# A two-layer graph network on one core: the search for low halves in the second batch, and the last batch's steps placed anew

## The chip, the cores and the metric

The kernel runs on one core of a Trainium2 chip. The metric is the device time of one launch in microseconds (us). One execution was recorded by the hardware profiler; all stretches of time in this document come from such records.

The names of the engines: PE is TensorE (matrix products), DVE is VectorE, ACT is ScalarE, POOL is GpSimd, and SP is SyncE, which here only issues DMA transfers. Each has its own queue of instructions and works through it in order.

## The reference

There are 32 batches of 512 rows with 512 columns, one 512x512 adjacency matrix of zeros and ones, and two layers, each followed by a residual and a normalisation of the rows.

```python
# layer 0: masked attention, 8 heads of 64
q = x @ Wq + bq; k = x @ Wk + bk; v = x @ Wv + bv
scores = einsum('bihd,bjhd->bhij', q, k) / sqrt(64) + where(adj == 0, -1e9, 0)
x = layernorm(x + einsum('bhij,bjhd->bihd', softmax(scores), v))
# layer 1: aggregation over neighbours, then a product
y = einsum('nm,bmd->bnd', adj, x)
x = layernorm(x + einsum('bnd,do->bno', y, weight) + bias)
```

## The kernel before, in words

All products of 512x512 matrices with a weight are made from seven products of halves instead of eight (a Strassen-like scheme: `FACTORS`, `ORDER`, L353 in `block_product`). One such product is one unit: `project(b, "q"/"k"/"v", i)` for the projections and `convolve(b, i)` for the product with the second layer's weight. A unit has 8 matmul records on PE, and its bank of PSUM is drained by DVE or ACT. Seven units make a whole product. Some of the sums of halves that go into them (`combine_rows`, L318) are made on POOL.

Attention runs in groups of four heads, two groups to a batch. For each group `attend` (L576) makes the weighted sum of values, `fold_squares` (L609, L611) adds up the exponentials on DVE, and `turn_out` (L592, L597) transposes the result on DVE into a tile named attT (two buffers) and sends it by 16 small DMA transfers into a tile of rows. `scores` (L552, L554, L556, L567) makes the scores of the next group: PE, then DVE adds the mask, ACT takes the exponential, POOL adds exponentials up. `scale_rows` (L635, ACT, 8 instructions for one pair of heads) and `add_rows` (L639, POOL) bring the result into the rows of x. In the last group of the last batch there are no rows by DMA: ACT copies into attT (L589), and `last_residual` (L645, L646, L648) turns it on PE and adds it on DVE.

The second layer takes y from the normalised rows. Each row tile is split into a high and a low half of reduced precision (L441 and L445; for the last batch by rows, `split_rows`, L486 on ACT and L487 on DVE), PE multiplies both with the adjacency (L472, for the last batch L499 in `aggregate_rows`), and ACT and DVE copy the banks to the tile yT (L475, L477; last batch L506, L504, L508). The adjacency itself must survive a reduction to the high half. `look_for_low_half` tests it, one block of rows at a time: ACT copies (L294) to a tile named high, DVE compares (L296) into a tile named attT, and reduces (L297). At the end `judge` joins this with two other measures (sums of exponentials and their inverses, gathered for each group by `add_up`), PE adds the verdict over the partitions (L864), and if it is bad, a general kernel runs after the fast one. With these inputs it does not run.

`statistics` (L415, L416) takes mean and variance of a block of 128 rows on DVE, `square_root` (L419, ACT), `invert_root` (L424, L425, DVE) and `normalise` (L430, ACT, one block of rows an instruction) make the normalisation. The last batch takes the statistics of the second layer by half rows (`half_statistics`, L837, closed in L854).

The order of work is written out by hand. `units_of(b)` returns two lists for a batch, one behind each of its groups of attention. `merge(units, behind)` places a list of small steps behind each PE unit: the k-th entry of `behind` follows the k-th unit. Work of four batches is in flight at once: while batch b is in attention, batch b+1 is projected, batch b-1 gets its first normalisation, splits and aggregation, and its second product comes up to a batch later; b-2 gets its second normalisation. After the loop over groups, a section written by hand ends the last two batches: t is B-1 = 31, `rest` the seven convolution units of t-1, `last` those of t. The order of the seven units is always 1, 2, 5, 6, 7, 3, 4.

Some tiles have few buffers, and a new use waits for the last reader of the old one: attT has two, high and low two each, k and q two each, yT one. Before, in the last batch, blocks 0 to 3 of `split_rows` share the two buffers of high and low. The unit `convolve(b, 7)` adds into the same MIX tile that unit 6 filled and that POOL reads.

Of the kernel before, what the change touches and what calls it, by code (L numbers as in the profile page):

```python
# [37 lines left out]
FP = mybir.dt.float32  # L38
FR = mybir.dt.float32r
# [168 lines left out]
def fast_kernel(ctx: ExitStack, tc, verdict, x, adj, Wq, bq, Wk, bk, Wv, bv, W1, b1, out):  # L208
# [3 lines left out]
    HP = H // 2  # L212
    NB = N // P
    DB = D // P
    assert N == 512 and D == 512 and H * HD == D
    root = float(HD) ** 0.5

    consts = ctx.enter_context(tc.tile_pool(name="consts", bufs=1))
# [199 lines left out]
    def square_root(t, slots):  # L418
        nc.scalar.activation(RSTD[t][:, slots], STAT[t][:, slots, 1], AF.Sqrt, bias=eps)  # L419

    def invert_root(t, slots):

        rstd = RSTD[t][:, slots]
        nc.vector.reciprocal(rstd, rstd)  # L424
        nc.vector.scalar_tensor_tensor(SHIFT[t][:, slots], STAT[t][:, slots, 0], -1.0, rstd,  # L425
                                       op0=ALU.mult, op1=ALU.mult)
# [25 lines left out]
    def store(b, blocks=None):  # L452
        for c in blocks or ():
            nc.sync.dma_start(out[b, c * P:(c + 1) * P, :], X[b][:, c, :])
        if blocks is None:
            nc.sync.dma_start(out[b].rearrange("(c p) d -> p c d", p=P), X[b])
# [23 lines left out]

    def split_rows(b, c):

        high = HIGH[b, c] = work.tile([P, D], FR, name="high")
        low = LOW[b, c] = work.tile([P, D], FR, name="low")
        row = X[b][:, c, :]
        nc.scalar.activation(high, row, AF.Copy)  # L486
        nc.vector.tensor_sub(low, row, high.bitcast(FP))  # L487

    def add_bias(b, c):
        nc.vector.tensor_add(X[b][:, c, :], X[b][:, c, :], b1_r)  # L490

    def aggregate_rows(b):

# [17 lines left out]
    def convolve(b, i):  # L511

        pm = bank(2, half)
        block_product(pm, YT[b], w1, i)
        x11, x12, x21, x22 = (X[b][:, 2 * r:2 * r + 2, s * half:(s + 1) * half] for r in range(2) for s in range(2))
        if i == 1:

            MIX[b] = work.tile([P, 2, half], FP, name="mix", tag="q" if b >= B - 3 else "low", bufs=2)
            nc.scalar.activation(MIX[b], pm, AF.Copy)
        if i in (6, 7):  # L520
            nc.vector.tensor_add(MIX[b], pm, MIX[b])
            for block in (x12,) if i == 6 else (x21, x22) if b == B - 1 else (x22,):
                nc.gpsimd.tensor_add(block, block, MIX[b])
        for block in {1: (x11,), 5: (x12, x22), 2: (x11,), 3: (x12,), 4: (x21,)}.get(i, ()):
            nc.vector.tensor_add(block, pm, block)  # L525
        if i == 4 and b < B - 1:

            nc.gpsimd.tensor_add(x21, x21, MIX[b])
# [6 lines left out]
    def convolution(b):  # L535
        return [(convolve, b, i) for i in (1, 2, 5, 6, 7, 3, 4)] if b >= 0 else []
# [104 lines left out]
    def last_residual(b, hp):  # L641

        pt = bank(NB, 2, HD)
        for c in range(NB):
            nc.tensor.transpose(pt[:, c, :, :], AT[b, hp][:, c * P:(c + 1) * P], ident)  # L645
        nc.vector.tensor_mul(pt, pt, inverse_of(b, hp)[:, :, :, None].to_broadcast([P, NB, 2, HD]))  # L646
        cols = X[b][:, :, hp * P:(hp + 1) * P]
        nc.vector.tensor_add(cols, pt.rearrange("p c s d -> p c (s d)"), cols)  # L648
# [15 lines left out]
    def run(units):  # L664
        for unit in units:
            unit[0](*unit[1:])
# [46 lines left out]
    def norm(t, which):  # L713

        if t - which < 0:
            return []
        lo, hi = which * NB, (which + 1) * NB
        return [(square_root, t, slice(lo, hi)), (invert_root, t, slice(lo, hi))] + [
            (normalise, t, slot) for slot in range(lo, hi)]
# [4 lines left out]
    def survey(b):  # L724

        return [(statistics, b, 1, c) for c in range(NB)] if b >= 0 else []
# [5 lines left out]
    def merge(units, behind):  # L732

        merged = []
        for k in range(max(len(units), len(behind))):
            merged += units[k:k + 1] + (behind[k] if k < len(behind) else [])
        return merged

    def units_of(b):

        made, turned = projections(b + 1), flips(b + 2)
        splits, gathered = aggregation(b - 1)
        old, seen = norm(b - 1, 1), survey(b - 2)

        fresh, young = ([(statistics, b - 1, 0, c) for c in range(NB)], norm(b - 1, 0)) if b else ([], [])
        scaled, added = residuals(b, 0)
        if b == B - 1:


            first, second = folds(b, 1)  # L750
            behind = [fresh[:2], fresh[2:], young[:1], young[1:3], young[3:5] + [first], young[5:] + splits[:1],
                      splits[1:]]
            return [merge(convolution(b - 2), behind), [second] + merge(gathered, [scaled, added, seen[:2], seen[2:]])]

        ready = [(turn_over, b)] if b > 1 else []
        if old:
            behind = [seen[:2], seen[2:], old[:2], old[2:4] + fresh[:2], old[4:] + ready + fresh[2:]] + [
                [u] for u in young]
        elif b:
            behind = [ready + fresh] + [[u] for u in young]  # L760
        else:
            behind = [[]] + [[(sum_weights, w1, n)] for n in range(4)]
        behind += [[] for _ in range(11 - len(behind))]
        behind += [splits[:1], scaled + added, splits[1:2]]
        slot0 = merge(made[:16], behind)
        values = made[16:]
        looked = [(look_for_low_half, c) for c in range(NB)] if b == 0 else []
        scaled, added = residuals(b, 1)
        slot1 = values[:3] + looked[:2] + gathered[:1] + splits[2:3] + gathered[1:2] + splits[3:] + scaled[:1]
        slot1 += values[3:] + looked[2:]  # L770
        if b == B - 2 > 0:
            slot1 += [(load, B - 1)]
        slot1 += gathered[2:3] + turned[:1] + gathered[3:]
        convolved = convolution(b - 1) if b < B - 2 else []
        slot1 += merge(convolved, [scaled[1:] + added[:1] + turned[1:2], turned[2:3], turned[3:4], [], [], [],
                                   added[1:] + turned[4:]])
        return [slot0, slot1]
# [31 lines left out]
    rest, last = convolution(t - 1), convolution(t)  # L809
    for hp in range(HP - PAIRS, HP):  # L810
        last_residual(t, hp)
    run(rest[:1])
    old, seen = norm(t - 1, 1), survey(t - 1)
    run(old[:1] + rest[1:2] + old[1:])
    if t > 1:
        store(t - 2)

    for c in range(NB):
        statistics(t, 0, c)
    ahead = norm(t, 0)  # L820
    run(ahead[:1] + rest[2:3] + ahead[1:2])
    for c in range(NB):
        run(ahead[2 + c:3 + c] + rest[3 + c:4 + c])
        split_rows(t, c)
    run(rest[3 + NB:])
    for c in range(NB):
        add_bias(t, c)
    aggregate_rows(t)


    halves = {}
# [2 lines left out]
    def half_statistics(c, s):  # L834
        if c not in halves:
            halves[c] = spare[:, c, :, :]
        nc.vector.bn_stats(halves[c][:, s, :], X[t][:, c, s * half:(s + 1) * half])  # L837

    old = norm(t, 1)
    beside = {1: seen, 2: old[:2], 5: old[2:3], 6: old[3:5], 7: old[5:]}  # L840
    for unit in last:
        run([unit] + beside.get(unit[2], []))
        if unit[2] == 2:
            well = judge()
        if unit[2] == 7 and t > 0:
            store(t - 1)
        for c, s in {2: ((0, 0), (1, 0)), 3: ((0, 1), (1, 1)), 4: ((2, 1), (3, 1), (2, 0), (3, 0))}.get(unit[2], ()):
            half_statistics(c, s)
            if (c < 2) == (s == 1):
                if t + 1 not in STAT:  # L850
                    for table, name, shape in ((STAT, "stat", (2 * NB, 2)), (RSTD, "rstd", (2 * NB,)),
                                               (SHIFT, "shift", (2 * NB,))):
                        table[t + 1] = work.tile([P, *shape], FP, name=name, bufs=3)
                nc.vector.bn_aggr(STAT[t + 1][:, NB + c, :], halves[c])  # L854
        ready = {3: (0, 1), 4: (2, 3)}.get(unit[2], ())
        if ready:
            slots = slice(NB + ready[0], NB + ready[1] + 1)
            square_root(t + 1, slots)
            invert_root(t + 1, slots)
            for c in ready:  # L860
                normalise(t + 1, NB + c)
                store(t, [c])
    pm = bank(N)
    nc.tensor.matmul(pm[0:1, 0:1], well, ones[:, 0:1], start=True, stop=True)  # L864
    nc.vector.tensor_scalar(verdict, pm[0:1, 0:1], P - 0.5, None, op0=ALU.is_lt)


# [22 lines left out]
```

## Time and profile before

| what | us |
|---|---|
| median of 3 runs (2759.68 to 2760.57) | 2759.97 |
| the profiled execution | 2760.76 |
| its span from first to last instruction | 2758.2 |
| PE busy | 2733.3 |
| POOL busy | 1898.7 |
| DVE busy | 2065.3 |
| ACT busy | 1411.5 |
| transfers of x and rows: SP issues an attT transfer, median until it lands | 1.8 |

A line of a timeline gives: start, duration, engine, line of the kernel, instruction, what is written and read with the shapes, how many instructions were merged, and in brackets how long the engine idled ahead of it and which event ended that. A line of waits gives: engine, tile and line that waited, for whom, then us in total, how many times, the longest. A line of stretches gives: from and to, length, busy us and number of instructions of PE, PE's weight loads, DVE, ACT and POOL, then the mean TensorE clock granted (1.00 is full), the share of the DMA engines and GB/s.

### The profile page before, as it was taken

Reading aid. Unit: us, or ns where it says so; the run is one execution under the profiler, and the core shown is the slowest. Engines: PE = TensorE matmul, PEld = TensorE weight load, DVE = VectorE, ACT = ScalarE, POOL = GpSimd, SP = SyncE. Lnnn points to the kernel's source line nnn. Section 1 sums busy time; section 2 is a strip of 40 time slices with the busy share of each in tenths; the row PEclk is TensorE's granted clock in tenths of the full one; section 3 lists DMA queues with packets and bytes.
Section 4 is the critical chain, followed back from the end, with each engine's and each line's share of the span. In section 5 each row is a group of like instructions: output and inputs, shape, how many; then the busy total and the mean of one; then the engine's idle time right before and its main releaser. Section 6 shows DMA issues by size and latency. Waiting matters only on the chain.

```text
span 2758.2 us, 39360 instructions
## 1 busy us (share of the span) xinstructions
PE 2733.3 (99%) x12856; PEld 1912.9 (69%) x12856; DVE 2065.3 (75%) x3351; ACT 1411.5 (51%) x2460; POOL 1898.7 (69%) x1220
## 2 busy tenths in 40 slices
PE   9999999999999999999999999999999999999997
PEld 6676766767767667677676676776766767767665
DVE  6778777777777777777877777777777777787777
ACT  3455554654545545446555465454554544655554
POOL 4666776767776668676677676777666867667774
PEclk9999999999999999999999999999999999999999
DMA  5112212222112222122221222211222212222111
GB/s 148 29 31 59 57 19 54 59 61 56 26 48 57 62 57 44 30 56 61 59 57 18 55 59 61 56 27 47 58 62 57 44 30 56 61 59 57 24 52 49
DMA packets 592915, 142.20 MB, mean 52 GB/s; under 512 B 554560, under 2 KB 558656, under 8 KB 592704
## 3 DMA queue, kind: packets, MB, share of 16 engines
q1 hardware_dynamic: 592704, 139.63, 22.9%
q8 instruction: 103, 1.69, 0.3%
q14 instruction: 108, 0.88, 0.1%
HBM read 72.88 MB, written 33.55 MB: 39 GB/s over the span
## 4 chain that ended last, share of the span: by engine, by line
PE 97%; DVE 1%; SPq 1%; ACT 0%; DMA 0%; issue 0%; POOL 0%; DVEq 0%; ACTq 0%
PE bank L353 55%; PE bank L552 16%; PE bank L576 16%; PE bank L472 8%; SPq L597 1%; PE bank L619 0%; DMA wq<-in_L_gnn_Wq_dram 0%; DVE bnst L415 0%; ACT rows L635 0%; PE bank L499 0%; DVE xT L525 0%; DVE part L837 0%; DVE xs L525 0%; DVE xT L490 0%; DVE stat L416 0%
## 5 line engine op out<-in xcount | busy, mean ns | idle before, releaser
L556 ACT ACTIVATE e<-e 128x1024 f32<-128x1024 f32 x512 | 524.5, 1052 | 579.8 <-DVE e L554 545.0
L554 DVE SCALAR_TENSOR_TENSOR e<-gap,bank 128x512 f32<-128x512 uint8 x1024 | 617.8, 678 | 20.6 <-PE bank L552 20.6
L567 POOL TENSOR_TENSOR es<-es,e 128x1024 f32<-128x1024 f32 x256 | 618.7, 2417 | 20.1
L567 POOL TENSOR_TENSOR es<-e 128x1024 f32<-128x1024 f32 x128 | 315.8, 2467 | 334.2 <-ACT e L556 334.2
L552 PE MATMUL bank<-q,k 64*128 64x512 f32 x2048 | 463.6, 598 | 0.0
L576 PE MATMUL bank<-e,v 128*64 128x512 f32 x2048 | 456.5, 598 | 4.7 <-DVE v L388 4.7
L353 PE MATMUL bank<-wv,xT 128*128 128x256 f32 x1792 | 405.4, 381 | 0.0
L353 PE MATMUL bank<-xT,wq 128*128 128x256 f32 x1792 | 400.8, 381 | 2.2 <-DMA wq<-in_L_gnn_Wq_dram 1.8
L353 PE MATMUL bank<-xT,wk 128*128 128x256 f32 x1792 | 402.9, 379 | 0.0
L353 PE MATMUL bank<-w,yT 128*128 128x256 f32 x1792 | 392.3, 379 | 0.5 <-DVE yT L504 0.5
L552 PEld LDWEIGHTS bank<-q,k 64*128 64x128 f32 x2048 | 203.1, 186 | 258.9 <-issue 149.2
L353 PEld LDWEIGHTS bank<-w,yT 128*128 128x128 f32 x1792 | 340.0, 190 | 48.3 <-DVE yT L504 0.9
L353 PEld LDWEIGHTS bank<-xT,wk 128*128 128x128 f32 x1792 | 340.2, 190 | 46.1
L353 PEld LDWEIGHTS bank<-xT,wq 128*128 128x128 f32 x1792 | 337.8, 190 | 49.1 <-issue 2.0
L353 PEld LDWEIGHTS bank<-wv,xT 128*128 128x128 f32 x1792 | 337.5, 190 | 47.6 <-DVE e L554 0.8
L635 ACT ACTIVATE rows<-rows,zero,inverse 128x64 f32<-128x64 f32 x1008 | 343.3, 426 | 0.0
L576 PEld LDWEIGHTS bank<-e,v 128*64 128x64 f32 x2048 | 142.2, 137 | 283.8 <-issue 282.7
L639 POOL TENSOR_TENSOR xs<-xs,rows 128x512 f32<-128x512 f32 x124 | 158.6, 1290 | 164.9 <-DMA xs<-in_x_dram 164.9
L556 ACT ACT_TABLE_LOAD x30 | 38.5, 1283 | 423.9 <-DVE e L554 423.9
L445 DVE TENSOR_TENSOR low<-xs,high 128x512 fp32r<-128x512 f32 x122 | 143.3, 1174 | 104.1 <-ACT high L441 104.1
L430 ACT ACTIVATE xs<-xs,shift,rstd 128x512 f32<-128x512 f32 x248 | 181.9, 803 | 32.3 <-DVE shift L425 32.3
L525 DVE TENSOR_TENSOR xs<-bank,xs 128x512 f32<-128x512 f32 x186 | 124.4, 683 | 97.0 <-PE bank L353 46.6
(123 smaller groups left out, 2963.5 us busy)
## 6 DMA issues: line engine op xcount, KB each, us to landing
rows<-attT SPq DMA_DIRECT2D x2016, 16.0 KB, 1.8
xin<-in_x_dram SPq DMA_DIRECT2D x496, 64.0 KB, 2.4
xs<-in_x_dram SPq DMA_DIRECT2D x31, 1024.0 KB, 5.1
out_dram<-xs SPq DMA_DIRECT2D x31, 1024.0 KB, 4.4
xin<-in_x_dram SPq DMA_DIRECT2D x4, 256.0 KB, 3.5
wq<-in_L_gnn_Wq_dram SPq DMA_DIRECT2D x2, 512.0 KB, 7.0
wk<-in_L_gnn_Wk_dram SPq DMA_DIRECT2D x2, 512.0 KB, 5.1
yT<-in_adj_dram SPq DMA_DIRECT2D x1, 1024.0 KB, 8.3
```

The source lines that it names most:

```text
L353: nc.tensor.matmul(pm[:, r, :], left[:, d, r * P:(r + 1) * P], right[:, d, :], start=(d == 0), stop=(d == 1))
L430: nc.scalar.activation(row, row, AF.Identity, bias=SHIFT[t][:, slot:slot + 1], scale=RSTD[t][:, slot:slot + 1])
L445: nc.vector.tensor_sub(LOW[b, d], cols, HIGH[b, d].bitcast(FP))
L472: nc.tensor.matmul(pm.rearrange("p a n -> p (a n)"), part, adjT[:, n % NB, :], start=(n == 0), stop=(n == 2 * NB - 1))
L525: nc.vector.tensor_add(block, pm, block)
L552: nc.tensor.matmul(ps[s], keys[:, j * P:(j + 1) * P], queries, start=True, stop=True)
L554: nc.vector.scalar_tensor_tensor(e[:, s, :], gap[:, j, :], NEG * root, ps[s], op0=ALU.mult, op1=ALU.add)
L556: nc.scalar.activation(e, e, AF.Exp, scale=1.0 / root)
L567: nc.gpsimd.tensor_add(ES[b, hp], ES[b, hp] if j > 1 else E[b, hp, 0], E[b, hp, j])
L576: nc.tensor.matmul(po[s * HD:(s + 1) * HD, :], values, e[:, s, :], start=(j == 0), stop=(j == NB - 1))
L635: nc.scalar.activation(part, part, AF.Identity, bias=zero, scale=inverse[:, c, s:s + 1])
L639: nc.gpsimd.tensor_add(cols, cols, ROWS.pop((b, hp)))
```

## The change

In words:

1. The four calls of `look_for_low_half` stood behind value projections in the second group of the first batch (b = 0). They now stand in the first group of the second batch (b = 1), behind the 8th to 11th projection unit.
2. In the first list of the last batch, the scaling of the rows of both pairs of heads moves forward: the first pair behind the square root for batch 30, the second behind the splits. In its second list the steps stand as [fold, both additions of rows, four aggregations]; the statistics of batch 29 are no longer there.
3. In the closing section the second normalisation of batch 29 (`old`) and its store move from ahead of the last batch's first statistics to beside the last batch's own convolution. The statistics of batch 29 (`older`) and `judge` now stand between the convolution of batch 30 and the copies of the last aggregation.
4. In `split_rows` blocks 2 and 3 take a buffer named k, each with room for high and low. The split of a block comes ahead of the convolution unit instead of behind it.
5. `add_bias` runs on POOL, not on DVE.
6. Unit 7 of the last convolution writes a new MIX tile.
7. Beside the last convolution: the second normalisation of batch 29 and half the statistics of batch 30 behind unit 1, the rest and the root of batch 30 behind unit 2, its four normalisations behind 5 and 6. The verdict's matmul and comparison follow unit 7. The statistics of blocks 2 and 3 of the last batch come after unit 4, and of these block 3 is normalised by one DVE instruction instead of one on ACT.

```diff
-        high = HIGH[b, c] = work.tile([P, D], FR, name="high")
-        low = LOW[b, c] = work.tile([P, D], FR, name="low")
+        if c > 1:
+            both = work.tile([P, 2, D], FR, name="k", bufs=2)
+            high, low = both[:, 0, :], both[:, 1, :]
+        else:
+            high = work.tile([P, D], FR, name="high")
+            low = work.tile([P, D], FR, name="low")
+        HIGH[b, c], LOW[b, c] = high, low
...
-        nc.vector.tensor_add(X[b][:, c, :], X[b][:, c, :], b1_r)
+        nc.gpsimd.tensor_add(X[b][:, c, :], X[b][:, c, :], b1_r)
...
-            nc.vector.tensor_add(MIX[b], pm, MIX[b])
+            mixed = MIX[b]
+            if i == 7 and b == B - 1:
+
+                MIX[b] = work.tile([P, 2, half], FP, name="mix", tag="q", bufs=2)
+            nc.vector.tensor_add(MIX[b], pm, mixed)
...
-            behind = [fresh[:2], fresh[2:], young[:1], young[1:3], young[3:5] + [first], young[5:] + splits[:1],
-                      splits[1:]]
-            return [merge(convolution(b - 2), behind), [second] + merge(gathered, [scaled, added, seen[:2], seen[2:]])]
+            behind = [fresh[:2], fresh[2:], young[:1] + scaled[:1], young[1:3], young[3:5] + [first],
+                      young[5:] + splits[:1], splits[1:] + scaled[1:]]
+            return [merge(convolution(b - 2), behind), [second] + added + gathered]
...
             behind = [ready + fresh] + [[u] for u in young]
+            behind += [[(look_for_low_half, c)] for c in range(NB)]
...
-        looked = [(look_for_low_half, c) for c in range(NB)] if b == 0 else []
         scaled, added = residuals(b, 1)
-        slot1 = values[:3] + looked[:2] + gathered[:1] + splits[2:3] + gathered[1:2] + splits[3:] + scaled[:1]
-        slot1 += values[3:] + looked[2:]
+        slot1 = values[:3] + gathered[:1] + splits[2:3] + gathered[1:2] + splits[3:] + scaled[:1]
+        slot1 += values[3:]
...
     run(rest[:1])
-    old, seen = norm(t - 1, 1), survey(t - 1)
-    run(old[:1] + rest[1:2] + old[1:])
-    if t > 1:
-        store(t - 2)
-
     for c in range(NB):
         statistics(t, 0, c)
     ahead = norm(t, 0)
-    run(ahead[:1] + rest[2:3] + ahead[1:2])
+    run(ahead[:1] + rest[1:2] + ahead[1:2])
     for c in range(NB):
-        run(ahead[2 + c:3 + c] + rest[3 + c:4 + c])
+        run(ahead[2 + c:3 + c])
         split_rows(t, c)
-    run(rest[3 + NB:])
+        run(rest[2 + c:3 + c])
+    run(rest[2 + NB:])
+    older, seen = survey(t - 2), survey(t - 1)
+    run(older)
     for c in range(NB):
         add_bias(t, c)
+    well = judge()
     aggregate_rows(t)
+    old = norm(t - 1, 1)
...
-    old = norm(t, 1)
-    beside = {1: seen, 2: old[:2], 5: old[2:3], 6: old[3:5], 7: old[5:]}
+    def close(c):
+        nc.vector.bn_aggr(STAT[t + 1][:, NB + c, :], halves[c])
...
+    next_ = norm(t, 1)
+    beside = {1: old + seen[:2], 2: seen[2:] + next_[:2], 5: next_[2:4], 6: next_[4:]}
+    upper, lower = slice(NB, NB + 2), slice(NB + 2, 2 * NB)
     for unit in last:
         run([unit] + beside.get(unit[2], []))
+        if unit[2] == 1 and t > 1:
+            store(t - 2)
         if unit[2] == 2:
-            well = judge()
-        if unit[2] == 7 and t > 0:
+            for c in range(2):
+                half_statistics(c, 0)
+        if unit[2] == 6:
             store(t - 1)
...
+        if unit[2] == 3:
+            for c in range(2):
+                half_statistics(c, 1)
+                close(c)
+            square_root(t + 1, upper)
+        if unit[2] == 7:
+            pm = bank(N)
+            nc.tensor.matmul(pm[0:1, 0:1], well, ones[:, 0:1], start=True, stop=True)
+            nc.vector.tensor_scalar(verdict, pm[0:1, 0:1], P - 0.5, None, op0=ALU.is_lt)
+    invert_root(t + 1, upper)
+    for c in range(2):
+        normalise(t + 1, NB + c)
+        store(t, [c])
+    for c in (2, 3):
+        half_statistics(c, 1)
+        half_statistics(c, 0)
+        close(c)
+    square_root(t + 1, lower)
+    invert_root(t + 1, lower)
+    normalise(t + 1, NB + 2)
+    row = X[t][:, 3, :]
+    nc.vector.tensor_scalar(row, row, STAT[t + 1][:, NB + 3, 0:1], RSTD[t + 1][:, NB + 3:NB + 4],
+                            op0=ALU.subtract, op1=ALU.mult)
+    store(t, [2, 3])
```

## The prediction

> **What bounds the kernel now.** I read the summary first: TensorE (PE) is busy 2733.3 of 2758.2 us, so only its gaps and its slow stretches can give time. Then the waits of PE alone. All that exceed 1.2 us, the start's weights apart, are two:
>
> ```profile
> PE bank L576 <- DVE v L388: 4.7, 1, 4.7
> PE bank L499 <- DVE low L487: 4.0, 1, 4.0
> ```
>
> (Columns: us in total, times, longest.) The rest of the 25 us is the tail after PE's last matmul (12.5 us). Third view, the timeline around the first wait, in the second group of the first batch:
>
> ```profile
> 120.87 1.94 PE L576 MATMUL bank<-e,v 128*64 128x512 f32 x8
> ...
> 124.65 0.79 DVE L296 TENSOR_TENSOR attT<-yT,high 128x512 f32<-128x512 f32 x1 [4.91 <-DMA rows<-attT]
> ...
> 127.50 8.04 PE L576 MATMUL bank<-e,v 128*64 128x512 f32 x24 [4.69 <-DVE v L388]
> ...
> 130.52 2.48 DVE L338 STREAM_TRANSPOSE xT<-xin 128x512 f32<-128x512 f32 x4
> ```
>
> look_for_low_half borrows an attT buffer whose rows are still leaving by DMA. VectorE (DVE) waits 4.91 us there, the values' drain (L388) is queued behind it, and PE waits. It costs more than the 4.69: the stretches of time show the TensorE clock (the figure after the engines) falling, and the scores coming late:
>
> ```profile
> 127.50:135.47 7.97, 7.97 (x24) 2.50 (x25) 7.87 (x11) 1.26 (x4) 5.76 (x5) 0.66 0.01 2
> 135.47:144.87 9.40, 9.40 (x35) 4.10 (x33) 9.37 (x14) 4.23 (x4) 5.02 (x4) 1.00 0.14 21
> 172.89:179.90 7.01, 7.01 (x33) 2.20 (x32) 6.22 (x6) 0.00 (x0) 0.95 (x1) 1.00 0.03 5
> 179.90:187.04 7.14, 7.14 (x35) 3.16 (x33) 6.69 (x11) 4.60 (x5) 1.24 (x1) 1.00 0.17 26
> ```
>
> The last two are the same work (attend, scores) one group later. From the first matmul of attend (120.87) to the end of scores (144.87) are 24.00 us against 14.15: **9.85 us lost**.
>
> Fourth, the end. The last batch's aggregation starts late and cold, and after PE's last matmul (2745.5) the DVE still has work:
>
> ```profile
> 2711.18 0.23 DVE L622 RECIPROCAL inverse<-bank 128x16 f32<-128x16 f32 x1
> ...
> 2723.23 0.47 PE L499 MATMUL bank<-adjT,low 128*128 128x512 f32 x1 [3.97 <-DVE low L487]
> ...
> 2733.68 11.92 PE L353 MATMUL bank<-w,yT 128*128 128x256 f32 x54 [0.45 <-DVE yT L504]
> ...
> 2751.68 1.52 ACT L430 ACTIVATE xT<-xT,shift,rstd 128x512 f32<-128x512 f32 x2 [0.49 <-DVE verdict L865]
> ```
>
> PE is idle from 2719.26. From 2723.23 its clock is 0.57 for 4 us and the matmuls start every 0.43 us, later every 0.23.
>
> **What the Trainium skill says.** (1) "TensorE: Matmul & The Clock Gate", What's actually happening: after an idle window of about 3.4 us the array runs at half clock, until about as long a busy window. The trace agrees: waits of 3.97 and 4.69 us are followed by clocks of 0.57 and 0.66, the wait of 0.45 us at 2733.68 is not. (2) "SBUF — State Buffer", SBUF: two separate sides: a GpSimd (POOL) instruction and a DVE instruction with two SBUF inputs lock each other out of one port pair for a whole instruction. The trace agrees even for a tiny one: L425 (128x4) takes 0.16 at 2715.78, where POOL idles, but here, with POOL's pair of additions running from 2686.26 to 2691.06,
>
> ```profile
> 2686.26 4.80 POOL L567 TENSOR_TENSOR es<-es,e 128x1024 f32<-128x1024 f32 x2
> ...
> 2690.47 0.61 DVE L425 SCALAR_TENSOR_TENSOR shift<-stat,rstd 128x4 f32<-128x4 f32 x1
> ```
>
> it ends at 2691.08, with POOL's. (3) "VectorE: DVE Perf Modes", The perf-mode tier table: an fp32 tensor_scalar from SBUF may run at twice the normal rate; no big one is in this trace.
>
> **Part 1, the four looks move from the first batch to the second.**
> - Removed: the wait, the cold matmuls, the late scores: 9.85.
> - What is next late there: the values' last drain would end near 121.7 (PE ends their matmuls at 120.87); the four transposes L338 take 2.48, to 124.2; folds and turns from 132.92 to 138.93 take 6.0, so the exponents' additions (L554) start at 130.2. In the later group they start 8.16 after attend does (172.89 to 181.06), here that is 129.05. They come 1.2 late. In the old run they came 2.3 later than usual and scores took 2.26 longer (9.40 against 7.14), one for one: **1.2 stays lost**.
> - Added in the second batch, behind units 8 to 11 of its first slot: per look on DVE 0.91 (L296) and 0.69 (L297), about 1.6, together 6.4; on ScalarE (ACT) 4 times 0.61. The drains there come each 1.73 us and take 0.69, so DVE has 1.04 free beside each; queued behind are drains, the splits' low halves and then folds. L296 has two SBUF inputs and meets POOL's additions (158.88 to 163.67), up to 1.4 of blocking once. Drain by drain I get the fold, at 174.01 before, begun 0.95 later; two waits on PE (0.34 at 180.02, 0.33 at 181.06) absorb 0.67. Bounds 0 (all hidden) to 1.8 (each low half also blocked for a POOL instruction); I take **0.7**. A gain is excluded: only work is added. The attT wait should not return: the 32 row transfers are issued until 156.7 and land 1.8 later, 158.5; the second look comes at about 162.
> - Sum: 9.85 - 1.2 - 0.7 = **8.0**.
>
> **Part 2, up to the last aggregation** (old time axis). Sixteen row scalings (L635, 5.41 us of ACT) went ahead of the yT copies. Eight now fill ACT's wait for the shift (2.27 us at 2688.91, they take 2.7: normalising 0.45 later), eight run behind the splits, till 2699.5. They hold up the attT copies until 2700.6; those are needed at 2706.08. Their two additions on POOL (L639) come in front of the yT combinations, but POOL is free at 2706.9. The last yT copy then ends 0.6 + 0.25 after PE's 2705.97, L477 at 2707.15. So L622 starts at 2707.15, not 2711.18 (the older batch's four statistics, 3.2, also left this place). On: L622 and L623 0.33, last_residual 2.7, one L525 0.6, four statistics 3.27: 2714.05. Before, low's end came 3.95 after that point (2719.14 to 2723.09), 0.62 of it a second L525 that is now elsewhere: **2717.4**. PE finishes its convolution at 2719.26, so it no longer waits, stays warm, and 32 matmuls at 0.232 end at 2726.7 instead of 2732.64. Blocks 2 and 3 have own buffers, so ACT's wait of 2.50 for high (2726.74) is gone too.
>
> **Part 3, what is late next: the yT copy on DVE.** From the first low (2716.6): low 0.6, two L525 1.2, low 0.6, L521 0.6, low 0.9, L521 after POOL's L523 at 2721.05, 0.6, low 1.1, L525 0.6 and 0.65: 2723.95. Now come the four older statistics, 3.16, and judge, 0.8, ahead of the copy (L504): 2727.9 without blocking. But the bias additions, 2.49 us of DVE before, are four POOL instructions now (1.27 each, 2725.3 to 2730.4), and judge holds two tensor_mul with two SBUF inputs. One lands inside a POOL instruction (half of 1.27), the next behind another (nearly all): I take 1.6; bounds 0 and 3.2 (judge cannot end later than the additions do). The copy ends 0.6 later: convolution starts at P = **2730.1** (2728.5 to 2731.7), against 2733.68. PE's idle time of about 3 us may or may not cool it.
>
> **Part 4, from P to the last store.** By DVE's queue: mix and first L525 end P+2.85; the older invert 0.25; statistics and drains to P+6.9; square root wait and invert 0.7; half statistics 0.65; L525 twice 1.2; two L521 1.25 (own MIX, so the second no longer waits 1.38); verdict 0.1; L525 waits for POOL's L523, to P+12.1; half statistics 1.2; L525 0.6; invert 0.35; four halves and two closings 1.8; root and invert 0.75; ACT normalises block 2 in 0.8, beside it DVE block 3 (0.35 to 0.7, hidden either way). That is P+17.6, last store issued at P+18.0 (SyncE needs 0.34 an issue). L425 beside POOL's combinations adds 0.6. So P+18.6 = 2748.7, before 2753.21 (P+19.5). Two stores at once in place of 0.8 apart cost 0.2 more. The older stores, moved behind these units, are issued 8 us before the end or more and land in 4.3: hidden. The verdict's matmul is hidden in PE's last units. Gain **4.3**.
>
> **Sum:** 12.3. The profiled execution took 2760.76 (span 2758.2): 2748.5. The median of the runs is 0.8 below it, 2759.97: **2747.7**.
>
> **Rivals.**
> A. The lock hardly bites in judge: P = 2728.5, tail gain about 6.3, second batch free: 15.0, **2745.0**. For it: a judge that falls between two POOL instructions isn't held. Against: the additions follow each other closely, and L425 at 2690.47. 0.18.
> B. The aggregation's gain turns into a wait at the copy: P = 2731.6 and PE cold, another 1.7 at the first convolution product: tail 1.1, with the dearer looks 8.0: **2752.0**. For it: idle would be nearly 4 us. 0.15.
> C. The first batch's loss isn't the looks' (the change doesn't do what it says), half of it stays: gain some 4.3, **2755.7**. Against: the wait names the attT transfer. 0.04.
> D. **Slower:** the second batch's looks meet the attT transfers in their turn. In the old place a wait of 4.91 cost 9.85, two for one. To lose all 12.3 and 5.5 more needs a wait of 8.9 at the second look: rows landing at 171 instead of 158.5. Nothing in SyncE's queue (xin loads come behind the rows) supports it: **2766**. 0.02.
>
> Main case 0.61, range of its own 2745.5 to 2750. My range takes A and B in: 2743.5 to 2753.0. What a measurement of this kernel can tell from no change is about 0.2%, 5.5 us (2754.5): faster 0.93, same 0.05, slower 0.02.
>
> **What would show it.** No wait of PE on L388; attend and scores near 120 to 145 us in about 15.3 us; L554 of the second batch's next group late by under 1. At the end no wait at L499, its matmuls 0.23 apart; a wait of 2 to 4 us at the first L353 behind them, on the copy; tensor_mul of judge taking about 1 us. Wrong if judge is short, if the clock falls before the last convolution, or if scores in the second batch take over 8.5 us.

## The result, and the profile after

The changed kernel takes 2749.17 us (median of 6 runs, 2748.99 to 2750.58), the kernel before beside it 2760.24 us (6 runs, 2759.59 to 2760.78). The ratio is 0.996, interval 0.995 to 0.9971: 11.1 us less, where 12.3 were forecast. The span of the profiled execution is 2747.3 us, 10.9 less. The changed kernel has other line numbers: attend is L585, scores L561, add_up's matmul L628 (L619 before), the last aggregation L504 with its copies in L511 (ACT) and L509 (DVE), the sums of the last convolution L534 and L530, judge L662 to L669.

The waits of PE in the changed kernel:

```profile
PE bank L353 <- DVE yT L509: 3.5, 1, 3.5
```

It is the only one over 1.2 us, the start's weights apart. Both large waits of before (4.7 on the values' drain, 4.0 on the low half) are gone. In their place stands one on the yT copy, which was 0.45. PE's timeline at the old place of the looks, and one group later, where they now stand ahead:

```profile
120.56 7.09 PE L585 MATMUL bank<-e,v 128*64 128x512 f32 x32
127.58 8.24 PE L561 MATMUL bank<-q,k 64*128 64x512 f32 x32
135.74 0.26 PE L628 MATMUL bank<-part,fold 128*32 128x16 f32 x8
...
163.76 7.09 PE L585 MATMUL bank<-e,v 128*64 128x512 f32 x32
170.77 7.69 PE L561 MATMUL bank<-q,k 64*128 64x512 f32 x32
178.40 0.26 PE L628 MATMUL bank<-part,fold 128*32 128x16 f32 x8
```

Attend is whole, and its 32 matmuls take 7.09 us in both places. From its start to the end of scores (the start of L628) are 15.18 us, against 24.00 before: 8.82 won. In the second batch it is 14.64 against 14.15: 0.49 given back. For what follows, from the kernel before, the add_up behind the second batch's scores, the last add_up, and the first matmuls of the last convolution:

```profile
187.04 0.26 PE L619 MATMUL bank<-part,fold 128*32 128x16 f32 x8
...
2705.89 0.26 PE L619 MATMUL bank<-part,fold 128*32 128x16 f32 x8
...
2732.64 0.59 PE L353 MATMUL bank<-w,yT 128*128 128x256 f32 x2
```

The end of the kernel in the changed profile, from the last group's add_up to the last convolution:

```profile
2698.29 0.26 PE L628 MATMUL bank<-part,fold 128*32 128x16 f32 x8
...
2699.37 0.25 DVE L631 RECIPROCAL inverse<-bank 128x16 f32<-128x16 f32 x1
...
2711.31 0.58 PE L504 MATMUL bank<-adjT,low 128*128 128x512 f32 x1
...
2717.44 4.96 POOL L495 TENSOR_TENSOR xT<-xT,b_r 128x512 f32<-128x512 f32 x4
...
2718.98 0.59 PE L353 MATMUL bank<-w,yT 128*128 128x256 f32 x2
...
2719.47 0.51 DVE L666 TENSOR_SCALAR well<-seen 128x2 f32<-128x2 f32 x1
...
2720.02 1.18 DVE L668 TENSOR_TENSOR well<-well 128x1 f32<-128x1 f32 x1
2721.22 1.18 DVE L669 TENSOR_TENSOR well<-well 128x1 f32<-128x1 f32 x1
2722.33 0.68 DVE L509 COPY yT<-bank 128x512 f32<-128x512 f32 x1
...
2723.07 10.16 PE L353 MATMUL bank<-w,yT 128*128 128x256 f32 x38 [3.49 <-DVE yT L509]
```

Read it with PE's last add_up as the zero point: 2698.29 here, 2705.89 before. The last aggregation begins at 13.0 instead of 17.3, with no wait. PE's first two matmuls of the last convolution stand at 20.7 instead of 26.8, so 6.1 us are won. Then judge: two multiplications of 128x1 take 1.18 us each while POOL's bias additions run, and the copy stands behind them. The second multiplication and the last addition end together, at 2722.40. The rest of the convolution starts at 24.8 instead of 27.8: of 6.1 us, 3.0 are left. And PE slows down after the wait, as the stretches of the changed kernel show (clock behind the five engines). In the first microsecond the clock is still full; over 3.93 us its mean is 0.66:

```profile
2723.07:2724.07 1.00, 1.00 (x5) 0.90 (x6) 1.00 (x3) 0.00 (x0) 0.00 (x0) 1.00 0.00 0
2723.07:2727.00 3.93, 3.93 (x12) 3.27 (x13) 2.65 (x7) 0.82 (x3) 2.59 (x3) 0.66 0.00 0
```

The last store is issued at 43.7 instead of 47.3, 3.6 us earlier; the span ends at 49.0 instead of 52.3, 3.3 us earlier.

The account of the two profiles: 0.3 from the first loads, 8.8 won and 0.5 given back by the looks, 1.0 lost spread over all later batches, 3.3 won at the end; together 10.9. The 1.0 is no single place: from the second batch's add_up to the last one are 2519.89 us instead of 2518.85. Add_up shifts by some 0.03 us from batch to batch, and within a batch it shows in the aggregation's matmuls. The first experiment shows which part of the change it belongs to.

### The profile page after: what moved, and what is told of

Read it like the earlier page. It is cut to its first block, busy times and chain, and to the rows that moved or that the text cites. A ratio compares the mean times of both kernels' runs of the same rounds, so it can differ in the third digit from the quotient of the medians.

```text
span 2747.3 us, 39383 instructions
## 1 busy us (share of the span) xinstructions
PE 2729.7 (99%) x12856; PEld 1911.3 (70%) x12856; DVE 2064.8 (75%) x3348; ACT 1411.4 (51%) x2459; POOL 1903.0 (69%) x1224
## 4 chain that ended last, share of the span: by engine, by line
PE 98%; DVE 1%; DMA 0%; ACT 0%; issue 0%; SPq 0%; POOL 0%; DVEq 0%; ACTq 0%
PE bank L353 56%; PE bank L561 17%; PE bank L585 16%; PE bank L472 8%; PE bank L628 0%; DMA wq<-in_L_gnn_Wq_dram 0%; DVE bnst L415 0%; DVE xs L534 0%; DVE part L847 0%; PE bank L287 0%; POOL xs L532 0%; SPq L239 0%; ACT xT L430 0%; DVE stat L416 0%; DVE xT L534 0%
## 5 line engine op out<-in xcount | busy, mean ns | idle before, releaser
L576 POOL TENSOR_TENSOR es<-es,e 128x1024 f32<-128x1024 f32 x256 | 618.3, 2415 | 20.1
L561 PE MATMUL bank<-q,k 64*128 64x512 f32 x2048 | 463.0, 598 | 0.0
L585 PE MATMUL bank<-e,v 128*64 128x512 f32 x2048 | 453.6, 595 | 0.0
L561 PEld LDWEIGHTS bank<-q,k 64*128 64x128 f32 x2048 | 203.4, 186 | 258.0 <-issue 152.2
L585 PEld LDWEIGHTS bank<-e,v 128*64 128x64 f32 x2048 | 141.4, 137 | 277.1 <-issue 275.7
L534 DVE TENSOR_TENSOR xs<-bank,xs 128x512 f32<-128x512 f32 x186 | 124.3, 682 | 96.8 <-PE bank L353 46.2
L430 ACT ACTIVATE xs<-xs,shift,rstd 128x512 f32<-128x512 f32 x248 | 181.9, 803 | 27.2 <-DVE shift L425 27.2
```

The costliest lines, as they stand in the source:

```text
L430: nc.scalar.activation(row, row, AF.Identity, bias=SHIFT[t][:, slot:slot + 1], scale=RSTD[t][:, slot:slot + 1])
L561: nc.tensor.matmul(ps[s], keys[:, j * P:(j + 1) * P], queries, start=True, stop=True)
L576: nc.gpsimd.tensor_add(ES[b, hp], ES[b, hp] if j > 1 else E[b, hp, 0], E[b, hp, j])
L585: nc.tensor.matmul(po[s * HD:(s + 1) * HD, :], values, e[:, s, :], start=(j == 0), stop=(j == NB - 1))
```

## The experiments

My theory was that the looks' place and the last batches' order are two gains that add, and that the second is cut short by POOL's bias additions, which hold judge up. The rivals stand in each expectation. The first four ran together, beside the kernel before at 2760.90 us; the other four beside it at 2760.76.

**The looks alone** (from the kernel before):

```diff
-        slot1 = values[:3] + looked[:2] + gathered[:1] + splits[2:3] + gathered[1:2] + splits[3:] + scaled[:1]
-        slot1 += values[3:] + looked[2:]
+        slot1 = values[:3] + gathered[:1] + splits[2:3] + gathered[1:2] + splits[3:] + scaled[:1]
+        slot1 += values[3:]
...
             behind = [ready + fresh] + [[u] for u in young]
+            behind += [[(look_for_low_half, c)] for c in range(NB)]
```

> The kernel before with one part of the change alone: the four looks for low halves stand in the second batch. My theory: this part is worth what PE's timeline shows of it (8.82 us won at attend and scores of the first batch, 0.49 given back at scores of the second), so 8.3 us less than before, about 2751.9 us. Rival: most of the gain belongs to the end of the kernel and this part gives under 5 us (2755 or more).

2753.04 us, 7.9 less; ratio 0.9971 (0.9959 to 0.9982). The theory holds within the interval, and the rival's 2755 or more is above all seven runs. PE's wait of 4.0 on the low half at the end is there as before. But the 8.3 is not all that this part does. Add_up in this run:

```profile
177.95 0.26 PE L619 MATMUL bank<-part,fold 128*32 128x16 f32 x8
...
2697.84 0.26 PE L619 MATMUL bank<-part,fold 128*32 128x16 f32 x8
```

Between the two lie 2519.89 us, as in the whole change, against 2518.85 before. All seven profiles with the looks in the second batch have 2519.88 to 2519.90 here; the last batches alone, the next run, has 2518.72, and the looks in their old place with another buffer have 2519.22. So the loss of 1.0 comes with the looks' move, and in the profiles this part is worth 8.3 - 1.0 = 7.3 us. Why the later batches are longer by 0.03 us each was not tried and stays open.

**The last batches alone** (from the changed kernel, the same lines the other way):

```diff
-            behind += [[(look_for_low_half, c)] for c in range(NB)]
...
+        looked = [(look_for_low_half, c) for c in range(NB)] if b == 0 else []
...
+        slot1 = values[:3] + looked[:2] + gathered[:1] + splits[2:3] + gathered[1:2] + splits[3:] + scaled[:1]
+        slot1 += values[3:] + looked[2:]
```

> The changed kernel with the four looks back in the first batch, so that only the last batches differ from before. My theory: 3.3 us less than before (the last store is issued 3.25 us earlier once the earlier shift is taken off), about 2756.9 us. Rival: the end is worth 6 us or more (2754 or less), and the parts do not add.

2757.03 us, 3.9 less; ratio 0.9985 (0.9978 to 0.9991). 7.9 and 3.9 make 11.8; the whole change made 11.1 and, repeated below, 10.5. The parts add, as closely as the intervals can tell. The 3.3 of the expectation is what the span's end shows in the two profiles, counted from add_up; the last store's issue comes 3.6 earlier. In this run's profile PE waits on the copy just as long as in the changed kernel, but does not slow down:

```profile
2731.80 8.47 PE L353 MATMUL bank<-w,yT 128*128 128x256 f32 x38 [3.53 <-DVE yT L509]
```

The 38 matmuls take 8.47 us, where they took 10.16. Yet from the last add_up (2707.05) to the span's end (2756.0) are 48.95 us, against 49.01 in the profile of the changed kernel above. It would be wrong to conclude that a slow PE costs nothing here: in that profile the clock was still full for the first microsecond, and the repetition of the changed kernel, the last run below, shows the other case.

**Looks in their old place, another buffer** (from the kernel before):

```diff
-        cut = work.tile([P, N], FP, name="attT")
+        cut = work.tile([P, N], FP, name="cut", tag="low")
```

> The kernel before, looks in their old place, but the comparison writes a buffer of the tag low instead of an attT buffer that a transfer still reads. My theory: the wait of 4.9 us goes and PE stays warm, but the 6.4 us of DVE work stay ahead of the transposes and folds, so the next scores come 4 to 5 us late: 5 us less than before, about 2755. Rival 1: the wait was all of it, 8.5 or more less (2751.7 or less). Rival 2: the wait was only where DVE's queue showed its length, and nothing is won (2759 or more).

2758.14 us, 2.8 less; ratio 0.999 (0.9983 to 0.9997). All three named too much or nothing; the gain is there, but only half of what I expected. PE and DVE in this run:

```profile
120.23 7.26 PE L576 MATMUL bank<-e,v 128*64 128x512 f32 x32
127.42 2.85 PE L552 MATMUL bank<-q,k 64*128 64x512 f32 x12
131.79 1.12 PE L552 MATMUL bank<-q,k 64*128 64x512 f32 x2 [1.52 <-DVE attT L592]
134.79 6.25 PE L552 MATMUL bank<-q,k 64*128 64x512 f32 x18 [1.88 <-DVE attT L592]
140.97 0.26 PE L619 MATMUL bank<-part,fold 128*32 128x16 f32 x8
```

```profile
123.48 2.13 DVE L296 TENSOR_TENSOR cut<-yT,high 128x512 f32<-128x512 f32 x1
```

The wait for the transfer is gone, and attend runs whole in 7.26 us. But scores now wait for banks that DVE hasn't drained: from attend to the end of scores 20.74 us pass. Of the 9.85 us that this place lost, the wait was worth 3.3 (24.00 to 20.74); some 5.6 is DVE work in a queue that PE stood behind (20.74 to 15.18). One comparison took 2.13 us here, beside POOL's additions. To give the looks another buffer in the same place would not have been enough; they had to leave DVE's queue there.

**Judge in a gap of DVE** (from the changed kernel):

```diff
     run(ahead[:1] + rest[1:2] + ahead[1:2])
+    well = judge()
...
-    well = judge()
     aggregate_rows(t)
```

> The changed kernel with judge moved up to the place where DVE waits 1.6 us for ACT's first high half and POOL is idle. My theory: judge (3.1 us, 2.3 of them held by POOL's bias additions) no longer stands ahead of the yT copy; its multiplications take under 0.2 us each, the wait of PE on the copy falls from 3.5 to about 0.4 and PE stays warm; 3 us less than the changed kernel, about 2746.1. Rival: the four older statistics and the chain behind set the end, and judge's place is worth its 0.8 us of work at most (2748.4).

2745.59 us; ratio to the kernel before 0.9946 (0.9933 to 0.996). That is 3.6 below the changed kernel's 2749.17 and 4.7 below its repetition, and all five runs (up to 2748.06) lie below all runs of the changed kernel (2748.77 and more). The theory holds; no version is faster, and the next one only equals it. Its timeline:

```profile
2707.01 0.16 DVE L668 TENSOR_TENSOR well<-well 128x1 f32<-128x1 f32 x1
...
2718.71 0.66 DVE L509 COPY yT<-bank 128x512 f32<-128x512 f32 x1
...
2719.42 8.47 PE L353 MATMUL bank<-w,yT 128*128 128x256 f32 x38 [0.36 <-DVE yT L509]
```

Both multiplications take 0.16 us where POOL is idle. PE waits 0.36, and 38 matmuls take 8.47 us, not 10.16. Counted from the last add_up (2697.78), the copy starts at 20.9 instead of 24.0, and the span ends at 45.8 instead of 49.0. The medians show more than these 3.2 us; what PE's clock adds is seen in the last run.

**The older statistics moved too** (from the last run):

```diff
-            return [merge(convolution(b - 2), behind), [second] + added + gathered]
+            return [merge(convolution(b - 2), behind), [second] + added + gathered[:2] + seen[:2] + gathered[2:3] + seen[2:] + gathered[3:]]
...
-    older, seen = survey(t - 2), survey(t - 1)
-    run(older)
+    seen = survey(t - 1)
```

> As the run with judge in the gap, and the four older statistics also leave the place ahead of the yT copy: they stand between the four aggregations of batch 30. My theory: the copy then waits for PE's last aggregation alone, so the last convolution starts about 0.5 us earlier than with judge moved alone (the copy was then ready to run 0.6 us late), but the 3.2 us of DVE work come ahead of the last batch's first statistics, where PE has 1.9 us to spare, and give some of it back: 0 to 1 us less than that run, 2745 to 2745.6. Rival: DVE's queue is the bound to the end, all 3.2 us are won: 2742.5.

2745.75 us, the same as with judge alone (2745.59): the theory's poor end, and far from the rival's 2742.5. The copy is made as soon as PE's banks are full:

```profile
2717.69 0.69 DVE L509 COPY yT<-bank 128x512 f32<-128x512 f32 x1 [1.07 <-PE bank L504]
...
2721.85 1.08 DVE L425 SCALAR_TENSOR_TENSOR shift<-stat,rstd 128x4 f32<-128x4 f32 x1
```

DVE waits 1.07 for PE, so PE is the bound up to here. Counted from add_up, DVE's first sum of the last convolution (L534) comes 0.6 earlier than in the run before; then L425 takes 1.08 us (0.61 there) beside POOL's combinations, and DVE's last instruction comes only 0.2 earlier. These statistics stand close to where the kernel before had them, between the aggregations of batch 30; with judge out of the way, their place makes no difference that these runs can show.

**Bias additions back on DVE** (from the changed kernel):

```diff
-        nc.gpsimd.tensor_add(X[b][:, c, :], X[b][:, c, :], b1_r)
+        nc.vector.tensor_add(X[b][:, c, :], X[b][:, c, :], b1_r)
```

> The changed kernel with the last batch's bias additions back on DVE, judge in its place. My theory: judge took 3.1 us because POOL's bias additions held it; without them it takes 0.8, and the 2.5 us of additions on DVE stand ahead of the copy instead: PE's wait on the copy stays 3.5 us within 0.4, and the time that of the changed kernel within 0.7. Rival: judge's length is its own, so the additions come on top: 2.5 us more than the changed kernel.

2749.82 us, the changed kernel beside it 2750.24: no difference. The theory holds:

```profile
2718.58 2.46 DVE L495 TENSOR_TENSOR xT<-xT,b_r 128x512 f32<-128x512 f32 x4
...
2721.63 0.16 DVE L669 TENSOR_TENSOR well<-well 128x1 f32<-128x1 f32 x1
2721.70 0.69 DVE L509 COPY yT<-bank 128x512 f32<-128x512 f32 x1
```

Judge takes 0.8 us again, the additions take 2.46, and PE's wait is 3.51 against 3.49. So the move of the bias to POOL won nothing with judge in this place: it took 2.5 us off DVE and put 2.3 back through judge. What it is worth with judge in the gap was not run.

**Blocks 2 and 3 in the shared buffers** (from the changed kernel; in effect the branch for own buffers is never taken):

```diff
-        if c > 1:
+        if c > NB:
             both = work.tile([P, 2, D], FR, name="k", bufs=2)
```

> The changed kernel with blocks 2 and 3 of the last batch's rows in the two shared buffers of high and low, as before. My theory: ACT's high of block 2 then waits until PE has read block 0 (near 2713 us of the changed kernel's profile, not 2710.8), and block 3's near 2715; PE itself hardly waits, but DVE's queue behind the low halves comes 1.5 to 2 us later, and so does the copy: 1.5 to 2 us more than the changed kernel. Rival: the wait is hidden by the POOL wait of the second L530 (1.19 us), nothing changes.

2752.90 us against 2750.24 beside it: 2.7 more. The direction is the theory's, the size larger. ACT stands idle 2.83 us before the high of block 2, which so comes 2.8 us later after add_up than in the changed kernel; the copies come 2.5 us later, and PE waits 5.5 us on them instead of 3.5:

```profile
2714.28 0.63 ACT L491 ACTIVATE high<-xT 128x512 fp32r<-128x512 f32 x1 [2.83 <-issue]
...
2726.28 11.19 PE L353 MATMUL bank<-w,yT 128*128 128x256 f32 x38 [5.49 <-DVE yT L509]
```

**The changed kernel once more.**

> The changed kernel itself once more, beside the others on the same chip: 11 us less than before, as the first time.

2750.24 us against 2760.76, ratio 0.9959 (0.9946 to 0.9973), 10.5 less. The profile of this repetition has the same wait of 3.49 us on the copy, at the same place after add_up (2697.76), and its 38 matmuls take 10.16 us as in the first one. But the clock falls sooner. In the convolution's first microsecond:

```profile
2722.53:2723.53 1.00, 1.00 (x3) 0.88 (x4) 1.00 (x3) 0.00 (x0) 0.00 (x0) 0.67 0.00 0
```

In the first profile that microsecond had 1.00. The first product of the convolution is therefore ready later, and DVE, which adds it up, waits longer. First in the first profile, then in the repetition:

```profile
2725.52 0.69 DVE L534 TENSOR_TENSOR xT<-bank,xT 128x512 f32<-128x512 f32 x1 [1.25 <-ACT mix L524]
```

```profile
2725.90 0.69 DVE L534 TENSOR_TENSOR xT<-bank,xT 128x512 f32<-128x512 f32 x1 [2.17 <-ACT mix L524]
```

From add_up that is 27.2 and 28.1 us. L425 behind it takes 0.91 instead of 0.60, and the span ends at 50.3 after add_up instead of 49.0. The two profiles differ in nothing that the program does, and the first difference at this end of the kernel is the clock: 0.9 us come with the first product, 0.3 with L425. So a slow clock costs some 1.3 us here when it takes in the first product, and next to nothing when it comes after it (49.0 with it, 48.95 in the last batches alone without it). This also fits the two distances of the run with judge in the gap: its end at 45.8 is 3.2 ahead of the first profile and 4.5 ahead of the repetition, as the medians are 3.6 and 4.7 apart. For the executions that were not profiled only a mean clock is on record, so for them this is not shown.

## Why the prediction was right, point by point

- **The loss at the old place** (9.85, of which 1.2 was to stay): 8.82 won, 1.03 stayed. DVE's transposes (L338) indeed come next, scores took 8.24 us. The number was right because it compared whole stretches, not the wait. The words around it were partly wrong: I put the transfer's wait first, and the run with another buffer shows it to be worth about a third; the larger share is 6.4 us of looks ahead of the folds.
- **The second batch** (0.7 to be given back): 0.49, by a partly lucky path. Two comparisons, not one, were held up beside POOL (1.92 and 1.53 us, where the other two took 0.68). The fold began 2.66 us after attend instead of 1.12, so 1.5 later and not 0.95; DVE's idle time in front of the scores, 0.94 us before and none after, took most of it up. No wait for attT there.
- **The batches behind it.** That the looks' move could cost anything there was put at nothing. It cost 1.0 us, so this part gave 7.3 in the profiles where 8.0 was forecast (7.9 in runs).
- **The last aggregation.** L622 was to start 4.0 us earlier: counted from add_up, its successor L631 starts at 1.08 instead of 5.29, 4.2 earlier. The end of PE's aggregation was to come 5.9 earlier: 6.1.
- **The copy.** Judge was given 0.8 + 1.6 (bounds 0 and 3.2 for the second); it took 3.1, so 2.3 was lost to the lock. The two multiplications took 1.0 each more, and a tensor_scalar, which I had not counted, 0.34 more. The prediction's own figures had a better answer: it let the additions end at 2730.4, 2.5 after judge's unblocked end at 2727.9, so its rule that judge cannot end later than they do gives a bound of 2.5, not 3.2, and judge in fact ended with them. The convolution was to start 3.6 us earlier, it started 3.0 earlier.
- **PE's clock**, which the prediction left open ("may or may not cool it") and priced in rival B alone, at 1.7: it fell in both profiles of the changed kernel, and cost next to nothing in one and 1.3 in the other.
- **From the convolution's start to the last store** 18.6 was worked out, 18.95 came in the first profile and 20.1 in the repetition; the own MIX, the parted statistics and block 3 on DVE (0.54 us, beside ACT's 0.81) did as said. Two stores together cost 0.3, not 0.2.
- So the end gave 3.3 in the first profile, 2.0 in the repetition and 3.9 alone in runs, not 4.3. The mis-sized terms are judge's lock (2.3 for 1.6, so 3.0 for 3.6 at the convolution's start), DVE's queue behind it (18.95 for 18.6, more where PE starts slow) and the stores (0.3 for 0.2). With 7.3 for 8.0 from the looks and 0.3 us of luck in the first loads, this makes the 10.9 of the first profile.
- **Rivals.** A failed by judge, C by the first experiment, D by the second batch's 0.49. B was half right: the aggregation's gain did turn into a wait at the copy, and the medians, 2749.17 and 2750.24, lie between the main case's 2747.7 and B's 2752.0. Two of the sums do not come out: A's gain at the end is 5.9 by its own figures (4.3 + 1.6), not 6.3; and the 4.3 of C is what is left if the looks give nothing, where half of their gain would leave 8 or so.

Of what the Trainium skill states, three things were used. The lock of "SBUF — State Buffer", SBUF: two separate sides, is borne out for the smallest instruction: 1.18 against 0.16 us. So is the idle window of "TensorE: Matmul & The Clock Gate", What's actually happening: 0.36 us of waiting doesn't cool, 3.49 does in the changed kernel; 3.53 in the last batches alone doesn't, and after the same 3.49 the clock fell sooner in the repetition, which fits a window that runs freely, as that section has it. For "VectorE: DVE Perf Modes", The perf-mode tier table, which gives twice the rate for rows of 2048, the one large fp32 tensor_scalar took 0.54 us against 0.68 of a tensor_tensor of the same shape, with rows of 512: faster, not twice as fast.

## What to carry to other kernels

Price a stalled place by a whole stretch against the same work elsewhere: a wait in the list of waits here showed 4.7 of 9.85 us, and removing its cause alone gave back a third. A step moved into the shadow of PE must leave the in-order queue that feeds PE, and small two-input DVE instructions should stand where POOL is idle: two of them cost 2.0 us more here beside POOL's additions. When work goes from one engine to another to relieve it, look at which instructions the new neighbour will hold up. And before a slow clock is called free, or a small gain real, profile the same kernel twice: here two profiles of one kernel differ by 1.3 us from the same point on.

## What the runs showed of the hardware

- A DVE multiplication of 128x1 with two SBUF inputs took 0.16 us or 1.18 us, by whether POOL was at a 128x512 addition. A tensor_scalar of 128x2 took 0.17 or 0.51 there.
- The end of the first group of attention lay at 78.32 us in the kernel before, and between 77.34 and 79.60 in the nine later profiles, whose code up to there is the same: the first loads move the whole by about 1 us from run to run.
- Waits of 3.5 us lie on the edge of slowing PE: after 3.49 us (twice) and 3.51 us 38 matmuls took 10.16, 10.16 and 10.08 us, after 3.53 in another run 8.47. After the same 3.49 us the clock's mean over the first microsecond was 1.00 in one profile and 0.67 in the other.
- PE can be held up and show no idle time at all. In the kernel before, the 32 matmuls of scores at 135.47 took 9.47 us with no gap, with the clock at 1.00 and DVE, which drains their banks, busy for 9.37 of 9.40 us; one group later they took 7.21.
